# Recommendation model on one core: the hand-over from the GRU to the AUGRU, with two key steps and the first gates moved ahead of the branch

## The chip, the core and the metric

The kernel runs on one core of a Trainium2 chip. A core has a matmul engine (TensorE, "PE" in the profile, with weight loads shown apart as "PEld"), a vector engine (VectorE, "DVE"), an activation engine (ScalarE, "ACT"), a general engine (GpSimd, "POOL") and a queue that issues transfers (SyncE, "SP"). The metric is the device time in microseconds (us) of one execution. The kernel before was timed in three runs: 2016.58, 2017.4 and 2022.05 us, median 2017.4.

## The reference

1024 users each have a history of 100 items of 128 values, a mask and a length. Cut to what matters:

```python
_, gru_seq = lax.scan(gru_step, h0, swapaxes(item_historical_embedding, 0, 1))
keys = swapaxes(gru_seq, 0, 1)                       # (1024, 100, 128)
q = broadcast_to(item_embedding[:, None, :], keys.shape)
feat = concatenate([keys, q, keys - q, q * keys], axis=-1)
score = mlp(feat, [(att_W0, att_b0), (att_W1, att_b1), (att_W2, att_b2)], relu)
attn = softmax(where(mask[:, :, None] == 1, score, -inf), axis=1)[..., 0]
pooled = einsum('bt,btd->bd', attn, keys)
att_seq = pooled.T[:T]                               # AUGRU's weights: step t uses pooled[:, t]
# AUGRU step, x_t = keys[:, t], a_t = att_seq[t]:
r = sigmoid([h, x_t] @ aug_Wr.T + aug_br)
u = a_t * sigmoid([h, x_t] @ aug_Wu.T + aug_bu)
h_hat = tanh([h * r, x_t] @ aug_Wh.T + aug_bh)
h = (1 - u) * h + u * h_hat
attention_feature = aug_out[b, sequential_length[b] - 1]
comb = concatenate([user, item, hist_sum, item * hist_sum, attention_feature], axis=1)
return mlp(comb, [(ph_W0, ph_b0), (ph_W1, ph_b1), (ph_W2, ph_b2)], sigmoid)[:, 0]
```

The AUGRU can't start before the softmax over all 100 steps is known, since its first weight is a column of `pooled`.

## The kernel before

Everything is float32. Values lie with the 128 features on the partitions and users along the free dimension, in two halves of 512 users (`HB`). The program has two parts: `gru_phase`, and after a branch `augru_phase`, of which three bodies exist for three tables of step widths. The number that chooses the body, `over_d`, is computed early in the GRU part and read by every engine when it reaches the branch.

**The loop of the GRU part** runs over the steps s = 0 to 99. In a step each half goes through `gru` (gates on PE, sigmoid and tanh on ACT, the state update on DVE), the previous state is transposed into a key tile `kt` on DVE (`transpose`) and stored to `keys_d` every four steps (`store`), and the attention net runs behind the recurrence: `attend(t)` is one round of PE work on four 32-column groups of the array, in which the first layer of step t, the second layer of step t - 1 and the third layer of step t - 2 run together, since `w12` holds the later layers in the column groups that the first layer leaves free. The first layer's input is `hn` (the key) and `kq` (key times item). Its item part is constant over the steps: it was computed once as `q0` (`item_part`), with the bias in it, and `take(t)` adds it: DVE writes `f = pm + q0` (line 734), ACT writes `mv = relu(f)` (line 739). `take` then sends the score row of step t - 2 to `s_b`, four copies for the four partition quarters, on the SP queue (line 746).

The softmax runs online in blocks that end at `ENDS`: the last three blocks are the steps 93 to 95 (called A here), 96 and 97 (B), 98 and 99 (C). Each block is three stages: `scores(0)` (transposes `s_b`, masks), `tops` (`scores(1)` and the running maximum), and, after the exponential on ACT (`exponents`), `sums` (mask, sum, the new denominator: lines 809 to 823). `pool` then rescales the accumulator `pooled` (line 626) and adds key times weight for each step (lines 636 and 637): for half 0 on POOL, for half 1 on DVE in the last stretch.

**The tail of the GRU part** follows the loop, written out by hand, from `gather_early(4)` on. It runs the attention rounds 99, 100 and 101 (`T` is 100), the softmax of A, B and C, and the last pooling. Between them stand: the eight parts of the prediction net's first layer that don't depend on the AUGRU (`features`, called `some(...)`: matmuls of line 667 on the first `next`, the copy of line 675 on the second; `features` 3 and 7 issue a store to `part_d`), the stores of the last key tiles (line 609), and indirect gathers of sorted key rows on POOL (`gather_early`, line 188). At the end DVE multiplies `pooled` with a mask into `s_b` (line 978), half 1 first, and SP writes it to `pooled_d`: columns 0 to 31 to `pooled_d[0]` (line 982), the other three quarters to `pooled_d[1]`: half 1's by SP (line 987), half 0's by ACT, in the AUGRU part (line 1410).

**The AUGRU part** begins on PE with the keys of steps 0 and 1, gathered long before as `rows[0, i]`: `load_key` transposes them on PE (line 1110) and copies them out on ACT (line 1111). `first_step` computes the gates of step 0, which need no state (lines 1030 and 1032). POOL gathers the sorted weights `att_r` from `pooled_d[0]`, four gathers for each half (`gather_weights`, line 153), and then the rows of two more blocks of keys (`load_row(1, 0, k)` for k = 14 and 15). PE spreads a weight column over the partitions (`weight_row`, line 1053, tiles `first` and `spare`), DVE makes the first state (lines 1064 and 1065), and the steps follow (`half_step`, lines 1127 and 1131 on PE). Later gathers of POOL are paced by a copy that waits for a state of the running step (line 187). `gather_more` takes the other three quarters of the weights from `pooled_d[1]` after step 4.

The queues matter here: each engine runs its instructions in the order of the program, SP issues its transfers in order, and POOL issues its gathers one after the other. PSUM banks of the tail: `banks` holds two for the softmax (`e`), one each for `kw` and `pt`, two for the features (`f`); the pool `pa` has two more, for the attention rounds.

Of the kernel before, what the change touches and what calls it, by code (L numbers as in the profile page):

```python
# [83 lines left out]
def kernel(ctx: ExitStack, tc: tile.TileContext, a: dict, out: bass.AP):  # L84
# [114 lines left out]
    def gru_phase(pools):  # L199
# [491 lines left out]
        def attend(t):  # L691
# [17 lines left out]

            for turn in range(2 * NH):  # L710
                i, j = divmod(turn, 2)
                for q in range(2):
                    first(i, q, j)
# [10 lines left out]
        def take(t):  # L724
# [6 lines left out]
            for half in halves:  # L731
                if t < T:
                    sums.append(wp.tile([P, HB], F32, name="f"))
                    nc.vector.tensor_add(sums[-1], p[half.i], q0[:, half.cols])
            for half in halves:
                half.mv = wp.tile([P, HB], F32, name="mv", bufs=4)
                to, of, bias = half.mv[rows, :], p[half.i][rows, :], bm[half.i][rows, :]
                if t < T:
# [19 lines left out]
        def softmax():  # L758
# [49 lines left out]
            def sums():  # L808
                nc.vector.tensor_mul(e[:, :, :n], e[:, :, :n], on)  # L809
                nc.vector.tensor_reduce(den_n, e[:, :, :n], AX.X, ALU.add)  # L810
                if j:
                    old = sp.tile([P, NK], F32, name="old")
                    nc.vector.tensor_mul(old, den_old, e[:, :, n])
# [120 lines left out]
        some(2, 3)  # L934
        take(T - 1)
        some(2, 3)
        attend(T)
        some(4)
# [3 lines left out]
        n = ENDS[-3] - ENDS[-4] + 1  # L942
        copy = banks["e"][0][:, : NK * n].rearrange("p (k n) -> p k n", n=n)
        nc.vector.tensor_copy(copy, weights[:, :, :n])
# [8 lines left out]
        some(4)  # L953
        attend(T + 1)
        some(5, 6)
        stage()
        take(T + 1)
        exponents()
        some(5, 6)
        some(7)  # L960
        for half in halves:
            half.store((T - 1) // G)
        halves[1].pool(T, nc.vector)
        stage()
        gather_early(3)
        halves[0].pool(T, nc.gpsimd)
        some(7)
        stage(2)
        exponents()
        stage()  # L970
# [15 lines left out]
        for to, t in later["att", 1]:  # L986
            nc.sync.dma_start(out=to, in_=t)

    def augru_phase(pools, widths, alive):
# [4 lines left out]
        fp = pools.enter_context(tc.tile_pool(name="fp3", bufs=NH))  # L994
# [24 lines left out]

        def first_step(i):  # L1020

            k = keys.pop((0, i))
            gates = []
            for j, (n, f) in enumerate((("u", AF.Sigmoid), ("h", AF.Tanh))):

                if j:
                    p = pa.tile([P, HB], F32, tag="a", name=f"p{n}")
                else:
                    p = bank(f"p{n}", FREE_BANK)
                nc.tensor.matmul(p, lhsT=later["w" + n][:, 1, :], rhs=k, start=True, stop=True)  # L1030
                gate = fp.tile([P, HB], F32, name=f"first_{n}")
                nc.scalar.activation(gate, p, f, bias=later["b" + n])
# [524 lines left out]
```

## Time and profile before

| what | value | from |
|---|---|---|
| median of the timed runs | 2017.4 us | times |
| the profiled execution | 2009.0 us, span 2007.1 us | times, page |
| PE, DVE, ACT, POOL busy | 99%, 83%, 47%, 63% of the span | page, part 1 |
| mean granted PE clock | 0.995 | cores |
| last gate matmul of the GRU loop starts | 1374.75 us | timeline of PE |
| first matmul of the AUGRU part (line 1110) | 1405.47 us | timeline of PE |
| first state gate (line 1131) | 1427.69 us | timeline of PE |
| AUGRU steps follow each other without a gap from | 1432.89 us | timeline of PE |
| 1378.7 to 1432.9 us: PE, DVE, ACT, POOL busy | 42.36, 35.38, 20.96, 41.37 of 54.20 us | stretches |

A busy share is an average over the whole span; the change touches only the stretch from about 1374 to 1433 us, 3% of it. There PE isn't busy throughout: it has the gap ahead of 1405.47 us and several waits after it. A line of the timeline gives the start in us, the duration, the engine, the line of the program, the operation, output and inputs, and how many instructions are merged; brackets hold the idle time ahead of it and what ended that. A line of the chain of waits gives the start, the duration and the work or transfer that the next piece waited for.

### The profile page before, as it was taken

To read this page: it belongs to the slowest core of one execution; us is meant where nothing else is said; L and a number is where in the kernel's file an instruction comes from. 1 tells how busy PE (TensorE), PEld (TensorE's weight loads), DVE (VectorE), ACT (ScalarE), POOL (GpSimd) and SP (SyncE) were. 2 spreads that over 40 slices of the span, in tenths; PEclk is the share of its full clock that TensorE was granted. 3 is DMA by queue.
4 is the path that set the end of the run, shared out by engine and by line. 5 is a ranking of instruction groups with operands and counts; after the bars stand their busy time and mean duration, and the time that the engine had idled before them with its cause. 6 is when DMAs were issued, how large, how long until landed. Compare 5 with 4: busy or idle time off the path is not lost. (4 is left out here: it accounts for less than half of the span.)

```text
span 2007.1 us, 41031 instructions
## 1 busy us (share of the span) xinstructions
PE 1983.7 (99%) x15380; PEld 994.6 (50%) x15380; DVE 1671.7 (83%) x3010; ACT 934.8 (47%) x1672; POOL 1274.2 (63%) x1325
## 2 busy tenths in 40 slices
PE   9999999999999999999999999998899999999998
PEld 2334444444444444444444444434444556678997
DVE  7878999887978888888878798998577777888985
ACT  4444454454544454544444454554343444444553
POOL 0233939669796959496896868898774353445331
PEclk9999999999999999999999999999999999999998
DMA  4443333333334434333333333333443343333331
GB/s 125 98 118 92 107 99 106 91 83 106 115 106 109 121 103 125 115 104 102 103 105 106 107 92 107 108 91 94 123 132 99 94 112 95 93 101 99 84 79 32
DMA packets 242075, 204.85 MB, mean 102 GB/s; under 512 B 59506, under 2 KB 204890, under 8 KB 241866
## 3 DMA queue, kind: packets, MB, share of 16 engines
q1 hardware_dynamic: 227514, 169.37, 30.2%
q0 software_dynamic: 12480, 32.04, 5.8%
q8 instruction: 123, 2.02, 0.4%
q10 hardware_dynamic: 1872, 0.72, 0.1%
q14 instruction: 86, 0.70, 0.1%
HBM read 146.01 MB, written 54.41 MB: 100 GB/s over the span
## 5 line engine op out<-in xcount | busy, mean ns | idle before, releaser
L534 PE MATMUL ps<-x,wih 128*32 128x512 f32 x4800 | 616.3, 593 | 0.0
L534 PE MATMUL ps<-hn,whh 128*32 128x512 f32 x4752 | 610.7, 592 | 1.4 <-ACT hn L582 1.4
L534 PEld LDWEIGHTS ps<-x,wih 128*32 128x32 f32 x4800 | 216.1, 110 | 302.0 <-issue 298.7
L534 PEld LDWEIGHTS ps<-hn,whh 128*32 128x32 f32 x4752 | 214.3, 110 | 298.9 <-issue 295.3
L519 POOL TENSOR_TENSOR xm<-x,m 128x512 f32<-128x512 f32 x200 | 234.9, 1174 | 143.2 <-DMA m<-mask_d 142.9
L546 ACT ACTIVATE r<-ps,brz 128x512 f32<-128x512 f32 x200 | 137.7, 689 | 386.3 <-PE ps L534 386.1
L520 POOL TENSOR_TENSOR hist<-hist,xm 128x512 f32<-128x512 f32 x200 | 257.9, 1290 | 15.7
L188 POOL DMA_INDIRECT rows<-keys_d,idx_k x218 | 211.5, 970 | 80.7 <-POOL rows L187 72.5
L637 POOL TENSOR_TENSOR pooled<-pooled,kw 128x512 f32<-128x512 f32 x191 | 245.0, 1283 | 15.0
L636 POOL TENSOR_TENSOR kw<-kt,e 128x512 f32<-128x512 f32 x191 | 206.2, 1080 | 69.7 <-DVE e L809 69.6
L565 ACT ACTIVATE ps<-ps,bih 128x512 f32<-128x512 f32 x200 | 132.4, 662 | 229.4 <-DVE ps L564 229.4
L700 PE MATMUL pm<-hn,wk 128*32 128x512 f32 x1200 | 221.8, 592 | 0.0
L700 PE MATMUL pm<-kq,wkq 128*32 128x512 f32 x1200 | 221.7, 592 | 0.0
L1139 ACT ACTIVATE c<-ph,bh 128x510 f32<-128x510 f32 (+57 forms) x174 | 88.3, 507 | 261.1 <-PE ph L1131 261.0
L554 DVE SCALAR_TENSOR_TENSOR u<-ps,bhh,r 128x512 f32<-128x512 f32 x198 | 147.5, 745 | 71.3 <-PE ps L534 68.6
L700 PE MATMUL pm<-mv,w 128*32 128x512 f32 (+1 forms) x808 | 195.4, 592 | 0.6 <-DVE e L790 0.6
L569 DVE TENSOR_TENSOR d<-hn,ps 128x512 f32<-128x512 f32 x198 | 136.1, 687 | 35.9 <-ACT ps L565 35.7
L564 DVE TENSOR_TENSOR ps<-ps,u 128x512 f32<-128x512 f32 x200 | 140.0, 700 | 25.9 <-remote 4.5
L582 ACT COPY hn<-ps 128x512 f32<-128x512 f32 x200 | 116.6, 583 | 93.5 <-DVE kq L576 91.8
L570 DVE TENSOR_TENSOR d<-ps,d 128x512 f32<-128x512 f32 x200 | 138.4, 692 | 26.0 <-ACT ps L566 11.6
L187 POOL COPY rows<-rest 128x1 f32<-128x1 f32 x202 | 38.4, 190 | 175.4 <-DVE rest L1168 170.0
L571 DVE TENSOR_TENSOR ps<-ps,d 128x512 f32<-128x512 f32 x200 | 139.9, 700 | 6.8
(224 smaller groups left out, 3111.8 us busy)
## 6 DMA issues: line engine op xcount, KB each, us to landing
x<-in_hist_x SPq DMA_DIRECT2D x210, 256.0 KB
keys_d<-kt SPq DMA_DIRECT2D x48, 1024.0 KB
m<-mask_d SPq DMA_DIRECT2D x200, 128.0 KB
rows<-keys_d,idx_k POOLq DMA_INDIRECT x218, 3.0
s_b<-mv SPq DMA_DIRECT2D x200, 8.0 KB
keys_d<-kt SPq DMA_DIRECT2D x32, 64.0 KB
mask_i<-in_mask SPq DMA_DIRECT2D x8, 200.0 KB
part_d<-part SPq DMA_DIRECT2D x2, 400.0 KB
```

What stands on the lines that cost most here:

```text
L188: nc.gpsimd.indirect_dma_start(out=r[:, at, :], out_offset=None, in_=keys_d[q], in_offset=bass.IndirectOffsetOnAxis(ap=idx_k[:, k, i : i + ...
L519: nc.gpsimd.tensor_mul(d, x, m)
L520: nc.gpsimd.tensor_add(acc, acc, d)
L534: nc.tensor.matmul(p[ts(q, R), :], lhsT=w[:, g, ts(q, R)], rhs=v, start=(j == 0), stop=(j == len(parts) - 1),)
L546: nc.scalar.activation(r, pr, AF.Sigmoid, bias=brz[:, 0:1])
L554: nc.vector.scalar_tensor_tensor(out=u, in0=ph, scalar=bhh[:, 2:3], in1=r, op0=ALU.add, op1=ALU.mult,)
L564: nc.vector.tensor_add(pi, pi, u)
L570: nc.vector.tensor_mul(d, pz, d)
L571: nc.vector.tensor_add(pi, pi, d)
L636: eng.tensor_mul(d, k, w)
L637: eng.tensor_add(acc, acc, d)
L700: nc.tensor.matmul(p[i][s, :], lhsT=w[:, s], rhs=v, start=start, stop=stop)
```

## The change

Four things are changed.

- **The attention rounds 98 and 99** (`T - 2 <= t < T`) get the item part as matmuls of `wq` and `item`, accumulated into the same PSUM tile (`query`: six more packs in a round, two for each half in the column groups 0 and 1, and one for each half in the group that `QB` names). `take` then no longer adds `q0` on DVE for these two rounds; ACT applies the bias and relu from PSUM.
- **The tail** is put in another order. Features are issued one at a time in other places (`some(2)`, `some(3)`, `some(4, 5)`, `some(6, 7)`), B's exponential comes ahead of `take(T + 1)`, half 1's pooling is cut in three (1, then 2, then the rest), `gather_early` runs 2 + 3 instead of 3 + 3 times, and the stores of the last key tiles come after the second part store. In A's `sums` the weights are first copied to PSUM, and the sum and the scaled old denominator are taken from there; the copy that stood after A's `sums` (line 944) goes.
- **The keys of steps 0 and 1** are transposed and copied in the tail, into `h3` and `hist`, and the **gates of step 0** are computed there, into `item` and the unused pair of `s_b`. `first_step`, its pool and the two key loads leave the AUGRU part.
- **The stores to `pooled_d[1]`** leave the hand-over: SP issues them in step 2 of the AUGRU, three after each half's step. One more key row gather (k = 13) comes behind the weight gathers.

```diff
--- before.py
+++ after.py
@@ -707,8 +707,17 @@
             def more(i, q):
                 pack(i, q, w12[i][k_rows, :], old[i][k_rows, :], True, q == QA[i] or t >= T)
 
+            def query(i, *groups):
+                for q in groups:
+                    pack(i, q, wq[i], item[:, halves[i].cols], False, False)
+
             for turn in range(2 * NH):
                 i, j = divmod(turn, 2)
+                if j and T - 2 <= t < T:
+                    query(i, 0, 1)
+                    if i:
+                        query(1, QB[1])
+                        query(0, QB[0])
                 for q in range(2):
                     first(i, q, j)
                 if i == 0:
@@ -729,13 +738,13 @@
             rows = slice(0 if t < T else 2 * R, P)
             sums = []
             for half in halves:
-                if t < T:
+                if t < T - 2:
                     sums.append(wp.tile([P, HB], F32, name="f"))
                     nc.vector.tensor_add(sums[-1], p[half.i], q0[:, half.cols])
             for half in halves:
                 half.mv = wp.tile([P, HB], F32, name="mv", bufs=4)
                 to, of, bias = half.mv[rows, :], p[half.i][rows, :], bm[half.i][rows, :]
-                if t < T:
+                if t < T - 2:
                     nc.scalar.activation(to, sums[half.i], AF.Relu)
                 else:
                     nc.scalar.activation(to, of, AF.Relu, bias=bias)
@@ -807,10 +816,17 @@
 
             def sums():
                 nc.vector.tensor_mul(e[:, :, :n], e[:, :, :n], on)
-                nc.vector.tensor_reduce(den_n, e[:, :, :n], AX.X, ALU.add)
+                f, old = e, None
+                if banks and both[1] is None:
+                    b = banks["e"][0]
+                    f = soft["copy"] = b[:, : NK * rows].rearrange("p (k n) -> p k n", n=rows)
+                    old = b[:, HB - NK :]
+                    nc.vector.tensor_copy(f, e[:, :, :rows])
+                nc.vector.tensor_reduce(den_n, f[:, :, :n], AX.X, ALU.add)
                 if j:
-                    old = sp.tile([P, NK], F32, name="old")
-                    nc.vector.tensor_mul(old, den_old, e[:, :, n])
+                    if old is None:
+                        old = sp.tile([P, NK], F32, name="old")
+                    nc.vector.tensor_mul(old, den_old, f[:, :, n])
                     nc.vector.tensor_add(den, den_n, old)
                 if last:
                     nc.vector.reciprocal(den, den)
@@ -931,17 +947,15 @@
         weights = soft["e"][0]
         exponents()
         some(0, 1)
-        some(2, 3)
+        some(2)
         take(T - 1)
-        some(2, 3)
+        some(2)
         attend(T)
-        some(4)
+        some(3)
         for half in halves:
             half.transpose(T - 1)
         stage()
-        n = ENDS[-3] - ENDS[-4] + 1
-        copy = banks["e"][0][:, : NK * n].rearrange("p (k n) -> p k n", n=n)
-        nc.vector.tensor_copy(copy, weights[:, :, :n])
+        copy = soft["copy"]
         for half in halves:
             half.todo = [
                 ((w[0], copy if w[0] is weights else None), n, t) for w, n, t in half.todo
@@ -950,23 +964,50 @@
         halves[1].pool(1, nc.vector)
         stage()
         take(T)
-        some(4)
+        some(3)
         attend(T + 1)
-        some(5, 6)
+        some(4, 5)
         stage()
+        exponents()
         take(T + 1)
-        exponents()
-        some(5, 6)
-        some(7)
+        some(4, 5)
+        some(6, 7)
+        halves[1].pool(1, nc.vector)
+        stage()
+        halves[0].pool(T, nc.gpsimd)
+        gather_early(2)
+        halves[1].pool(2, nc.vector)
+        some(6, 7)
+        for n in range(2):
+            for half in halves:
+                k = (h3[half.i], hist[:, half.cols])[n]
+                p = pa.tile([P, HB], F32, tag="a", name="pk")
+                for g in range(GH):
+                    nc.tensor.transpose(
+                        p[:, ts(g, P)], rows[0, half.i][:, g, ts(n, P)], ident
+                    )
+                nc.scalar.copy(k, p)
+                later["key", n, half.i] = k
         for half in halves:
             half.store((T - 1) // G)
-        halves[1].pool(T, nc.vector)
-        stage()
-        gather_early(3)
-        halves[0].pool(T, nc.gpsimd)
-        some(7)
         stage(2)
         exponents()
+        for half in halves:
+            gates = (item[:, half.cols], s_bs[NH * ((soft["j"] - 1) % 2) + half.i])
+            later["gates", half.i] = gates
+            for to, (n, f) in zip(gates, (("u", AF.Sigmoid), ("h", AF.Tanh))):
+                if half.i:
+                    p = banks["f"].pop(0)
+                else:
+                    p = pa.tile([P, HB], F32, tag="a", name=f"p{n}")
+                nc.tensor.matmul(
+                    p,
+                    lhsT=later["w" + n][:, 1, :],
+                    rhs=later["key", 0, half.i],
+                    start=True,
+                    stop=True,
+                )
+                nc.scalar.activation(to, p, f, bias=later["b" + n])
         stage()
         halves[0].pool(T, nc.gpsimd)
         halves[1].pool(T, nc.vector)
@@ -983,15 +1024,12 @@
             later["att", half.i] = [
                 (others[p - 1], t[p * R : (p + 1) * R]) for p in range(1, P // R)
             ]
-        for to, t in later["att", 1]:
-            nc.sync.dma_start(out=to, in_=t)
 
     def augru_phase(pools, widths, alive):
 
 
 
         qp = pools.enter_context(tc.tile_pool(name="qp3", bufs=4 * NH))
-        fp = pools.enter_context(tc.tile_pool(name="fp3", bufs=NH))
         wp = pools.enter_context(tc.tile_pool(name="wp3", bufs=3))
         sp = pools.enter_context(tc.tile_pool(name="sp3", bufs=2))
         kp = pools.enter_context(tc.tile_pool(name="kp3", bufs=4))
@@ -1016,22 +1054,6 @@
                 n = ring.pop(0)
                 ring.append(n)
             return ps[n].tile([P, HB], F32, tag="g", name=name)
-
-        def first_step(i):
-
-            k = keys.pop((0, i))
-            gates = []
-            for j, (n, f) in enumerate((("u", AF.Sigmoid), ("h", AF.Tanh))):
-
-                if j:
-                    p = pa.tile([P, HB], F32, tag="a", name=f"p{n}")
-                else:
-                    p = bank(f"p{n}", FREE_BANK)
-                nc.tensor.matmul(p, lhsT=later["w" + n][:, 1, :], rhs=k, start=True, stop=True)
-                gate = fp.tile([P, HB], F32, name=f"first_{n}")
-                nc.scalar.activation(gate, p, f, bias=later["b" + n])
-                gates.append(gate)
-            return gates
 
         def gather_weights(i):
             r = wp.tile([P, GH, P], F32, tag="att_r", name="att_r", bufs=2)
@@ -1401,15 +1423,10 @@
             return [b - a for a, b in zip(done, done[1:])]
 
 
-        for i in range(NH):
-            load_key(0, i, (None, FREE_BANK)[i])
-        gates = [first_step(i) for i in range(NH)]
-        for i in range(NH):
-            load_key(1, i, (FREE_BANK, None)[i])
-        for to, t in later["att", 0]:
-            nc.scalar.dma_start(out=to, in_=t)
+        gates = [later["gates", i] for i in range(NH)]
+        keys.update({(1, i): later["key", 1, i] for i in range(NH)})
         sorted_rows = [gather_weights(i) for i in range(NH)]
-        for k in range(14, KH):
+        for k in range(13, KH):
             load_row(1, 0, k)
         for i in range(NH):
             load_key(2, i, (FREE_BANK, None)[i])
@@ -1438,6 +1455,9 @@
                     whole_step(t)
                 for _ in range(due.pop(0) if due else 0):
                     next(ahead, None)
+                if t == FIRST[1] - 2:
+                    for to, of in later["att", i]:
+                        nc.sync.dma_start(out=to, in_=of)
                 if t > FIRST[1]:
                     next(more, None)
                 if t == FIRST[2]:
```

## The prediction

> **What bounds the kernel now.** I read the chain of waits first, since it says which part of the hand-over sets the end. In order of time (start, duration, work) it begins so:
>
> ```profile
> 1427.23 3.61 DMA att_r<-pooled_d,idx
> ...
> 1430.89 0.50 PE spare L1053 x2
> ...
> 1432.89 1.12 PE pr L1131 x2
> ```
>
> The last of the eight weight gathers lands at 1430.84 us, PE spreads the weight, DVE makes half 1's state, and from 1432.89 all the rest of the chain is PE. So a shift of this landing is a shift of the end, one for one. What ended the waits ahead of it stands in the timelines of POOL and SP:
>
> ```profile
> 1411.35 1.27 POOL L637 TENSOR_TENSOR pooled<-pooled,kw 128x512 f32<-128x512 f32 x1
> ...
> 1415.32 0.95 POOL L188 DMA_INDIRECT rows<-keys_d,idx_k  x1 [0.30 <-DMA rows<-keys_d,idx_k]
> 1418.45 0.95 POOL L153 DMA_INDIRECT att_r<-pooled_d,idx  x1 [2.17 <-DMA pooled_d<-s_b]
> ```
>
> ```profile
> 1397.13 3.22 SPq L609 DMA_DIRECT2D keys_d<-kt  x2
> 1400.44 5.13 SPq L677 DMA_DIRECT2D part_d<-part  x1
> 1413.55 0.93 SPq L982 DMA_DIRECT2D pooled_d<-s_b  x2
> ```
>
> POOL was free at 1416.27 and waited for the two writes of `pooled_d[0]`, the second issued at 1414.15 (1413.55 and 0.6 on). These wait for DVE's last two products, and DVE's timeline shows it closed from 1386.46 on:
>
> ```profile
> 1386.46 1.29 DVE L734 TENSOR_TENSOR f<-pm,q 128x512 f32<-128x512 f32 x2 [1.52 <-PE pm L700]
> ...
> 1389.31 1.02 DVE L813 TENSOR_TENSOR old<-den,e 128x32 f32<-128x32 f32 x1
> 1390.37 1.29 DVE L814 TENSOR_TENSOR den<-den,old 128x32 f32<-128x32 f32 x1
> ...
> 1393.90 0.72 DVE L786 STREAM_TRANSPOSE last<-s_b 128x512 f32<-128x512 f32 x1
> ...
> 1400.65 0.71 DVE L786 STREAM_TRANSPOSE last<-s_b 128x512 f32<-128x512 f32 x1
> ...
> 1412.83 1.29 DVE L978 TENSOR_TENSOR s_b<-used,pooled 128x512 f32<-128x512 uint8 x2
> ```
>
> So the hand-over is DVE's line of work, then a write, then eight gathers. Beside it PE has a path of its own:
>
> ```profile
> 1389.81 1.91 PE L700 MATMUL pm<-mv,w 128*32 128x512 f32 x8
> ...
> 1405.47 1.94 PE L1110 MATMUL pk<-ident,rows 128*128 128x128 f32 x8 [6.10 <-issue]
> ...
> 1424.92 1.16 PE L1053 MATMUL first<-ident,att_r 128*128 128x128 f32 x8 [0.72 <-ACT k L1111]
> ```
>
> It stands 6.10 us at the branch, and its first weight spread waited for a key copy, not for a gather: this path is nearly as long as the other.
>
> **Step 1, the item part on PE.** Round 100's row above holds two packs after each other in each of two column groups: 1.91 us, 0.85 a pack and 0.2 to drain. The six new packs put two more on groups 0 and 1, so a round gets 1.7 us longer; bounds 0.85 (the second pair runs beside others) and 2.55 (three batches). Round 98 starts at 1374.35 and the features behind it at 1378.70, now 1380.4; they take 2.9 (to 1381.61), so round 99 starts at 1383.3. It took 4.74 (1381.61 to 1386.35), with a wait for `mv`, which ACT finished at 1382.69; that is now early. Unhindered it is 4 x 0.85 + 0.2 = 3.6, with the packs 5.3: it ends at 1388.6, 2.25 later than before.
>
> **Step 2, what DVE is spared.** Four `f` adds (1381.94 - 1380.74 and the row of 1386.46): 2.5 us, and the 1.52 of waiting. A's `sums` with the copy took from 1388.89 to 1391.86, 2.97 us; the two small products in it lasted 1.02 and 1.29, while B's on PSUM operands took 0.19 each. With the copy at 0.28 the new one is 1.3 us: 1.7 less. DVE ends its last loop product at 1380.82, the first stages of A (3.0) at 1383.8, ACT loads its table and takes the exponential (1.6, both key transposes beneath it) to 1385.5, `sums` to 1386.8, one pooling piece (2.1) to 1388.9. From there B's scores could start, 5.0 us ahead of 1393.90.
>
> **Step 3, where PE takes it back.** B's scores need the row of step 97, out of round 99. ACT takes relu straight from PSUM (1.26 by the rows of rounds 100 and 101): 1388.7 to 1389.95, where before it ended at 1388.42. The write before was issued for half 1 at 1388.44 and moved its last bytes at 1389.8 (transfers in slices of 0.1 us). So half 0's row is there at 1390.9: B starts at 1391.1, 2.8 ahead of before, after 2.2 us of idle DVE. Ends: 1388.9 to 1392.8.
>
> **Step 4, to the last product.** B's two stages take 3.04 (1393.90 to 1396.94), one pooling piece 1.44, B's `sums` 1.1, two pieces and a rescale 3.55: C's scores at 1400.3. Its row is ready: rounds 100 and 101 end at 1391.95 and 1395.3, the relu at 1396.65, the write at 1398.1. C's stages 3.04, exponential 0.3, `sums` 1.93: 1405.6, only 0.3 ahead of 1405.92, since 3.5 us of half 1's pooling now stand ahead of it. POOL takes B at 1396.9 (5.82, as from 1400.89 to 1406.71), two gathers 2.5, C at 1405.7 (5.83): half 0 is pooled at 1411.5, 1.1 earlier. DVE ends half 1 at 1410.6 and waits for POOL; the last product ends at 1412.3, 1.8 earlier than 1414.12.
>
> **Step 5, write and gathers.** From the second write to the first gather took 4.3 us (1414.15 to 1418.45). With 4.3 again the gathers start at 1416.65, 1.8 earlier. POOL is done with its three row gathers at 1415.1 and would allow 3.3. The six writes to `pooled_d[1]` are out of the way, which speaks for less than 4.3; the key stores, moved from 1397 to about 1401.8, speak for more. Transfers were at 90% or more from 1398.3 to 1408; shifted and short of one gather that is 1402.6 to 1412, and SP, whose next issue behind two stores took 5.13 us, is free again by then. I keep 4.3; ends 2.8 and 6.5 (the landing of a row gather in that full stretch). Eight gathers take 8.78 from first to last start, and the last lands 2.5 to 3.6 later (the seven others, the chain's row): 1427.9 to 1429.0.
>
> **Step 6, PE's path.** Features 6 and 7 end at about 1400.7, the four keys with their copies (0.45 and 0.58 each) at 1403.2, four gates at 0.86 at 1406.6: all this lies under DVE's line and costs nothing unless PE arrives late. It then meets the branch: 6.1 us as before, with transfers as full as before, so 1412.7. From the keys of step 2 to the first weight spread it took 9.2 us (1415.72 to 1424.92). The stretches show the clock that part of this will run at (PE, PEld, DVE, ACT, POOL, clock, transfers, GB/s):
>
> ```profile
> 1401.90:1405.40 3.50, 0.00 (x0) 0.00 (x0) 2.85 (x13) 0.23 (x1) 3.38 (x4) 0.50 1.09 322
> 1405.40:1408.00 2.60, 1.94 (x8) 1.57 (x8) 2.50 (x6) 0.00 (x0) 2.49 (x3) 0.50 0.88 273
> 1408.00:1412.10 4.10, 2.97 (x4) 1.29 (x5) 3.94 (x6) 3.04 (x4) 3.94 (x4) 0.50 0.04 14
> 1412.10:1415.00 2.90, 2.84 (x9) 1.09 (x8) 1.98 (x3) 1.84 (x3) 2.45 (x3) 0.99 0.17 37
> ```
>
> Half speed came 2.5 us after PE's last matmul and lasted until 6.6 us after its first. The same after the new gap, at a busy share of 0.75 (4.91 of 6.7 us), costs 6.6 x 0.75 / 2 = 2.5: first spread at 1424.4. From it to the spread for half 1 took 5.0 (1424.92 to 1429.94): 1429.4. Ends: 1426.9 without any slow clock, 1429.7 with all 6.6 us busy.
>
> [...]
>
> **The small moves.** The six writes at step 2 cost SP some 3.6 us (1.88 for three, ACT's 1.69). Behind them on SP wait only weight loads for two steps later, with 10.1 us a step (half 0's gate at 1444.53 and 1454.62). The one more row gather is 1.26 of POOL after the eighth; POOL then stood idle 3.86 until 1434.56. Without that cover it costs 1.26.
>
> **Sum.** The start of the closed run follows the later of 1427.9 to 1429.0 and 1429.4: 1429.4 against 1430.84, 1.4 us less. The profiled execution took 2009.0 (span 2007.1): 2007.6. The timed median is 8.4 above the profiled execution; that offset kept, 2017.4 - 1.4 = 2016.0. The ends of steps 3, 5 and 6 together give -3.3 to +0.6: 2014.1 to 2018.0.
>
> **Rivals.** *DVE's line comes through whole*: packs at the low end, B at 1388.9. Then POOL is bound by its own work (1394.8 after A, 5.82, 2.5, 5.83: 1409), and the branch must be shorter as well. Some 4 us less: 2013.4. For it: the 5.0 of step 2 are sure; against: round 99 and PE's path. *No change*: PE's branch and slow clock, or the same landing, keep 1430.8; within 0.6 of 2017.4. For it: the 0.72 row, where PE was late already. *Slower, by the moved key stores*: they still fill the transfers when `pooled_d[0]` is written. A write that then takes as long as a row gather in the full stretch, 6.5 instead of 2.6, starts the gathers at 1420.5, 2.1 after before: 2019.5. It decides from where the stores last beyond about 1414; 1412 is my sum, so it is near. Against: some 4 us of quiet transfers between 1409.5 and the first write at 1413.55 before.
>
> **Numbers.** Forecast 0.5, whole line 0.14, no change 0.22, slower 0.14. A difference of 0.3%, 6.05 us, is about what a measurement of this kernel can tell from no change; no case reaches it alone, but the timed runs spread by 5.5 us. Faster than 2011.3: 0.10, within: 0.82, slower than 2023.4: 0.08. Range 2011 to 2021: the cases' ends 2013.4 and 2019.5, and some 2 us of that spread.
>
> **What would show it.** Right: 12 more records in rounds 98 and 99, no `f` in the tail, DVE idle ahead of B's first transpose at about 1391, the small sums at 0.2, the first weight gather near 1416.6, and PE closed from about 1431.5. Wrong: B's first transpose without a wait (step 3), transfers at 90% beyond 1413 (step 5), the gap at PE's branch under 4 us or the first weight spread waiting for a gather (step 6), a stall in steps 2 to 5.

## The result and the profile after

| | before | after |
|---|---|---|
| median of 14 runs each | 2019.01 us (2016.58 to 2022.05) | 2018.73 us (2015.81 to 2021.3) |
| ratio, 95% interval | | 0.9998 [0.9991, 1.0005] |
| profiled execution, span | 2009.0, 2007.1 us | 2018.55, 2016.7 us |
| granted PE clock of that execution | 0.995 | 0.993 |

No difference could be measured: -0.3 us, with an interval from -1.8 to +1.0. The kernel before took about 2019 us in three of the five series of runs here and about 2007.6 us in the two others, and its first profile (2009.0 us) is near the second, so a time is compared only with before's in its own series. In the traces I count from a common point, the last gate matmul of the GRU loop (1374.75 us before, 1374.83 after).

The chain of waits of the kernel after, in order of time (start, duration, what), goes over PE, ACT and the branch ("issue"), where that of before went over the last weight gather:

```profile
1401.43 0.67 PE pk L986 x4
...
1407.25 3.86 issue
1411.11 1.94 PE pk L1132 x8
...
1421.24 0.58 ACT k L1133
...
1424.72 1.12 PE pr L1153 x2
...
1427.98 0.59 ACT at L1092
...
1432.34 0.66 DVE att_t L1100
...
1434.39 1.12 PE pr L1153 x2
```

No transfer is on it any more: the tail is quicker, and the weights are there when PE asks. The first state gate starts at 1424.72 (before 1427.69), yet the closed run (the stretch from which PE's steps follow each other without a gap) starts at 1434.39, 1.5 us after before's 1432.89. So 3.0 us were won, and 4.5 lost in the first half step.

DVE's timeline shows the tail:

```profile
1385.81 0.30 DVE L824 COPY last<-e 128x128 f32<-128x128 f32 x1
...
1386.44 0.20 DVE L829 TENSOR_TENSOR last<-den,last 128x32 f32<-128x32 f32 x1
...
1390.64 0.73 DVE L795 STREAM_TRANSPOSE last<-s_b 128x512 f32<-128x512 f32 x1 [1.86 <-DMA s_b<-mv]
...
1403.43 0.23 DVE L818 TENSOR_TENSOR last<-last,on 128x64 f32<-128x64 f32 x1 [1.06 <-ACT last L815]
...
1412.07 0.69 DVE L1019 TENSOR_TENSOR s_b<-used,pooled 128x512 f32<-128x512 uint8 x1 [1.16 <-POOL pooled L637]
```

The copy and the short sums are as cheap as on PSUM before (0.30 and 0.20, where before had 0.28 and 0.19 there; `old` took 1.02), B's first transpose waits 1.86 us for its row, and the last product waits for POOL. One wait is new: C's products wait 1.06 us for ACT, whose exponential stands behind the copies of the moved keys.

SP's queue and POOL's timeline show the write and the first gather:

```profile
1401.18 3.12 SPq L609 DMA_DIRECT2D keys_d<-kt  x2
1410.94 2.18 SPq L1023 DMA_DIRECT2D pooled_d<-s_b  x2
```

```profile
1415.18 0.95 POOL L188 DMA_INDIRECT rows<-keys_d,idx_k  x1 [0.30 <-DMA rows<-keys_d,idx_k]
1416.44 0.95 POOL L153 DMA_INDIRECT att_r<-pooled_d,idx  x1 [0.30 <-issue]
```

The first weight gather (1418.45 before, behind a wait of 2.17 for the write) follows POOL's own gathers of rows with 0.30 between, as they follow each other. PE's timeline shows its own path:

```profile
1382.59 0.62 PE L700 MATMUL pm<-hn,wk 128*32 128x512 f32 x2
...
1386.51 1.42 PE L700 MATMUL pm<-kq,wkq 128*32 128x512 f32 x6
...
1411.11 1.94 PE L1132 MATMUL pk<-ident,rows 128*128 128x128 f32 x8 [4.59 <-issue]
...
1421.87 1.23 PE L1075 MATMUL first<-ident,att_r 128*128 128x128 f32 x8 [0.67 <-ACT k L1133]
```

Round 99 is bounded by the first two. The gap at the branch is 4.59 us where it was 6.10, and the first weight spread still waits for the copy of a key, not for a gather.

What eats the gain stands side by side in the timelines of PE and ACT in the first half step:

```profile
1425.67 1.02 PE L1153 MATMUL pu<-h_all,wu 128*128 128x510 f32 x2
1426.53 0.60 PE L1098 MATMUL pw<-ident,att_r 128*32 128x128 f32 x4
1428.62 1.16 PE L1075 MATMUL spare<-ident,att_r 128*128 128x128 f32 x8 [1.49 <-ACT at L1092]
```

```profile
1427.98 0.58 ACT L1092 COPY at<-spare 128x512 f32<-128x512 f32 x1 [6.16 <-PE pw L1098]
1429.39 0.66 ACT L1173 ACTIVATE pr<-pr,br 128x510 f32<-128x510 f32 x1 [0.82 <-PE spare L1075]
1432.18 0.66 ACT L1174 ACTIVATE pu<-pu,bu 128x510 f32<-128x510 f32 x1 [2.14 <-PE ph L1153]
```

ACT's sigmoid of `pu` starts at 1432.18, 5.5 us after the matmuls of `pu` ended (1426.69), and ACT had been idle 2.14. Its copy of `spare` starts 4.0 us after the spreads that it reads. The semaphore records of PE agree: ten of its signals come within 0.35 us from 1432.16 on. PE's signals, not its matmuls, are late there. "Late signals" below means this: engines that wait for PE start microseconds after its matmuls have ended.

### The profile page after: what moved, and what is told of

It is laid out like the page before. It is cut to its first block, busy times and chain, and to the rows that moved or that the text cites. A ratio compares the mean times of both kernels' runs of the same rounds, so it can differ in the third digit from the quotient of the medians.

```text
span 2016.7 us, 41069 instructions
## 1 busy us (share of the span) xinstructions
PE 1989.9 (99%) x15404; PEld 1006.2 (50%) x15404; DVE 1666.0 (83%) x3006; ACT 934.0 (46%) x1672; POOL 1277.2 (63%) x1325
## 4 chain that ended last, share of the span: by engine, by line
PE 96%; DVE 2%; ACT 1%; issue 1%; DVEq 0%; ACTq 0%
PE ps L534 49%; PE pm L700 17%; PE ph L1153 5%; PE pr L1149 4%; PE pr L1153 4%; PE pu L1153 4%; PE ph L1149 4%; PE pu L1149 4%; PE last L667 1%; PE pr L1226 0%; PE ph L1226 0%; PE pu L1226 0%; PE p L1313 0%; PE p L1308 0%; PE p L1354 0%
## 5 line engine op out<-in xcount | busy, mean ns | idle before, releaser
L1177 DVE TENSOR_TENSOR pu<-pu,c 128x510 f32<-128x510 f32 (+57 forms) x173 | 81.9, 473 | 77.9 <-ACT c L1161 71.9
```

## The experiments

The runs were taken in four series after the comparison above: first `r_before`, `r_after`, `gates_only` and `gates_back`, one timed run each; then `swap_banks`, `late_state`, `rows_behind` and `swap_and_rows`; then `after_5`, `swap_early_rows` and `swap_banks_2`; last `gates_back_5`. In the later three each changed kernel has 11 timed runs.

The main numbers, in us from the GRU's last gate matmul (starts of the second write to `pooled_d[0]`, the first weight gather, the first weight spread, then of state gates, in the last two columns half 0's):

| kernel | write | gather | spread | step 1, half 0 | step 1, half 1 | step 2 | step 11 |
|---|---|---|---|---|---|---|---|
| before | 39.40 | 43.70 | 50.17 | 52.95 | 58.14 | 64.69 | 152.57 |
| r_before | 39.44 | 43.89 | 50.64 | 53.41 | 60.23 | 66.77 | 154.65 |
| after | 37.96 | 41.61 | 47.04 | 49.89 | 59.56 | 66.11 | 153.99 |
| r_after | 37.97 | 41.63 | 47.43 | 50.48 | 60.72 | 67.83 | 155.71 |
| after_5 | 37.97 | 41.62 | 47.16 | 49.94 | 54.77 | 61.31 | 149.19 |
| gates_only | 40.52 | 45.04 | 50.62 | 53.39 | 61.34 | 70.73 | 158.61 |
| gates_back | 37.19 | 40.85 | 54.49 | 58.27 | 63.13 | 69.68 | 157.56 |
| gates_back_5 | 37.19 | 40.85 | 54.54 | 58.32 | 64.94 | 71.49 | 159.37 |
| swap_banks | 37.95 | 41.61 | 47.94 | 50.71 | 55.10 | 61.65 | 150.49 |
| swap_banks_2 | 37.96 | 41.61 | 48.29 | 51.06 | 55.45 | 62.00 | 150.82 |
| late_state | 37.96 | 41.62 | 47.76 | 53.47 | 61.09 | 67.63 | 155.51 |
| rows_behind | 37.96 | 41.26 | 47.63 | 50.40 | 55.23 | 61.78 | 151.44 |
| swap_and_rows | 37.96 | 41.62 | 47.77 | 50.54 | 54.93 | 61.48 | 151.37 |
| swap_early_rows | 37.96 | 41.62 | 47.92 | 50.69 | 55.08 | 61.63 | 149.51 |

**1. Both kernels once more.** No edit.

> The kernel before once more, for a profile beside that of the kernel after. Two spans are counted from the last gate matmul of the GRU loop: to the first state gate of the AUGRU (52.9 us in the first profile) and to its closed run, the first PE work behind the first state of half 1 (58.1 us). If the hand-over is the same in every execution, both repeat within 0.3 us. If it varies from run to run by more than 1 us, the difference of 1.5 us between the two profiles says nothing.

> The changed kernel once more. Its profile has the first state gate 49.9 us after the loop and the closed run 59.6 us after it: 3.0 us won and then 4.5 us lost in the first half step, in which ACT and DVE start some 4 us after PE's matmuls have ended. Theory 1, the loss belongs to the new order: both spans repeat within 0.3 us. Theory 2, it is an accident of that execution: the first span repeats, the closed run comes at 55.0 us, 5.1 after the first state gate as in the kernel before.

One run each, 2016.08 and 2018.52 us, beside 2019.94 for another run of before: too few to rank. Up to the gathers each kernel repeats itself within 0.2 us, and the first state gate of the change is 2.9 us earlier (50.48 against 53.41). From it to half 1's took 10.24 us in the change; in the kernel before 6.82, where its first profile has 5.19. So the late signals aren't the change's own: a second profile of before has them as well, for less time. The gain up to the first state gate repeats, and half 1's gate isn't earlier.

**2. The moved gates alone, on the kernel before.**

```diff
+        for n in range(2):
+            for half in halves:
+                k = (h3[half.i], hist[:, half.cols])[n]
...
-        gates = [first_step(i) for i in range(NH)]
+        gates = [later["gates", i] for i in range(NH)]
```

> The kernel before with one part of the change alone: keys of steps 0 and 1 and the gates of step 0 ahead of the branch. DVE's line of work is that of before. If that line and the gathers behind it set the start, the first state gate stays at 52.9 and the closed run at 58.1, within 0.5 us. If PE's own path set it (its first weight spread waited 0.72 us for a key copy), up to 0.7 us are won. If the new entry itself brings the late half step of the changed kernel, the closed run is some 9.5 us after the first state gate instead of 5.2.

2021.42 us in one run, beside 2019.94 for before. The first state gate is no earlier than before's (53.39), and half 1's is 3.2 us later than in the first profile of before, with late signals. But the write, 1.1 us later than before's, was late already ahead of everything that was moved. Round 99's last matmul ended at 1385.42, and DVE's sum of it began 1.2 us after that, where before it took 0.11:

```profile
1386.62 1.29 DVE L734 TENSOR_TENSOR f<-pm,q 128x512 f32<-128x512 f32 x2 [2.67 <-PE pm L700]
```

PE's time saved is then spent waiting: 2.93 us for a copy of a key, which ACT made behind its three stores to `pooled_d[1]` (issued from 1414.31 on), and these wait for DVE's last product. So DVE's line holds this start, but how much the moved gates would win without the 1.1 us can't be read from this one profile. The trace of before gives a bound: its fourth weight gather starts at 1422.21, the gathers land 2.4 to 2.6 us after their start, so half 0's last weights are there at about 1424.7 (an estimate), and the spread that needs them ran from 1424.92 to 1426.08. A shorter path of PE alone could win about 1 us there, not 3.

**3. The change without the moved gates.** The same diff the other way round, on the kernel after: its tail, with the keys and the first gates behind the branch.

> The changed kernel with the keys and the first gates back behind the branch, all else as changed. The weight gathers start some 1.9 us earlier than before, but PE has its old path behind the branch: if that path binds, the first state gate is at 52.5 to 53 us, and the closed run at 57.5 to 58.1. If the gathers alone bind, 50 to 51 and 56. If the late half step comes from the tail or the stores and not from the entry, it is here too: 9.5 us from the first state gate to the closed run.

> The changed kernel with the keys of steps 0 and 1 and the first gates put back behind the branch, once more, timed: the tail is then as quick as in the changed kernel, and PE's own work behind the branch is that of before. Theory D (what binds the first state gate is the later of two lines: the tail with its weight gathers, and PE's own keys and gates behind the branch; the change shortens both and neither alone pays): the second write at 37.2 us from the GRU's last gate matmul as in the changed kernel, the first spread at 50 to 54.5 behind PE's own work with no wait for a gather, half 0's first state gate at 53 to 58 (before 52.95, changed 49.9), time 0 to 3 us over the kernel before. Rival (the tail alone binds, and PE's moved keys only fill idle time): first spread at 47 to 48, the gate at 50 to 51, time 1 to 3 us below before as with the whole change.

One run of 2017.58 us, and timed later 2021.56 against 2018.63, ratio 1.0015 [1.0006, 1.0024]: 2.9 us slower, beyond its interval. The write is 2.2 us earlier than in before and the gathers 2.9, but the first spread is at 54.5 in both profiles, 4 us later than before's. PE's timeline of the second, and a row of ACT's, show for what it waits:

```profile
1408.69 2.08 PE L1043 MATMUL pu<-k,wu 128*128 128x512 f32 x2 [5.71 <-ACT k L1124]
...
1425.62 0.66 PE L1123 MATMUL pk<-ident,rows 128*128 128x128 f32 x4 [1.84 <-issue]
1427.82 1.55 PE L1066 MATMUL first<-ident,att_r 128*128 128x128 f32 x8 [1.54 <-ACT k L1124]
```

```profile
1407.57 1.07 ACT L1124 COPY k<-pk 128x512 f32<-128x512 f32 x2 [6.48 <-issue]
```

It waits for its own keys; the last of the eight gathers had started at 1422.91. But this isn't before's path of PE with a shorter tail: the first copy of a key stands on ACT 6.48 us behind its last work, with no wait that the profile shows, and PE's first gate waits 5.71 us for it (1.73 in before); the half clock lasts 13.7 us (10.2 in before). So half 0's gate is at 58.3, 5 us later than the 52.5 to 53 that the first expectation gave to a binding path of PE. What the runs and the bound above show is that each line holds the start when only the other is shortened: the shorter tail with the old entry gives nothing, the moved gates alone at most about 1 us, and both together bring the first gate 3 us forward. Why ACT's copy comes so late there stays open.

**4. Step 1 with two uses of a bank exchanged.** On the kernel after:

```diff
-                store_weights(0, pa.tile([P, HB], F32, tag="a", name="pw"))
-                first_state(1, spare)
+                first_state(1, pa.tile([P, HB], F32, tag="a", name="first"))
+                store_weights(0, spare)
```

> The changed kernel with two of step 1's uses of a PSUM bank exchanged: half 1's first-state weights are spread into the bank that half 0's first state has just left, and the transposes for the store of half 0's weights go into the bank `spare`. In the changed kernel PE's spread for half 1 stands behind a copy on ScalarE (of `spare` into `at`) that began 4.0 us (5.8 in the repeat) after PE had ended what it reads. All spans from the last gate matmul of the GRU. Theory A (the first half step is long because half 1's spread waits for that copy, and VectorE's copy of `pw` stands ahead of half 1's state): half 1's first state gate, at 59.6 and 60.7 in the two profiles of the changed kernel, comes some 5 to 6 us behind half 0's (49.9 and 50.5), so at 55 to 57, and the kernel is 3 to 5 us quicker than the changed one. Theory B (what PE has done is told late to the other engines at this place of the program, whatever the order): ACT and DVE begin step 1's sigmoids and products 3 to 6 us after the matmuls they read, half 1's gate stays at 58.5 to 61, and the time is within 1.5 us of the changed kernel's 2018.7.

> The exchange of banks alone once more, beside the other two: half 1's first state gate 0.3 to 0.6 us earlier than in the changed kernel where the signals aren't late, time 0 to 1.5 us below it. If the late signals show in this call, the gate is at 58 to 61 in all three, and the exchange didn't remove them.

Ratios 0.9993 [0.9984, 1.0002] and 0.9998 [0.9989, 1.0007]. In both series the late signals were gone from every profile, in that of the unedited kernel too (run 5), so these runs can't say whether the exchange would cure them. What it gives without them: 4.39 us from gate to gate in both against 4.83 in `after_5`, so 0.4 us, not the 3 to 5 that theory A expected from the first profiles. And it was given back: PE waits in step 4, and DVE's timeline shows the cause:

```profile
1457.11 1.10 PE L1149 MATMUL pr<-k,wr 128*128 128x496 f32 x2 [0.69 <-DVE k L1139]
```

```profile
1456.34 1.30 DVE L1139 STREAM_TRANSPOSE k<-rows 128x512 f32<-128x512 f32 x2 [2.40 <-DMA rows<-keys_d,idx_k]
```

A gather of rows is late. POOL issues one per 1.44 us, each paced by a copy of `rest`, which DVE makes later here, behind half 1's state: the first paced copy is at 57.3 us from the common point, in `after_5` at 56.4.

**5. The change itself, without late signals.** No edit.

> The changed kernel once more, to see where its gain goes on a chip on which the signals of PE aren't late (or to see them late again). All spans from the last gate matmul of the GRU. Theory C (the gain is real up to step 1, and POOL's gathers of rows take part of it back before step 4): first state gate of half 0 at 50.4, of half 1 at 55.0 to 55.5 (52.95 and 58.14 in the profile of before), PE waits 0.7 to 1.8 us for VectorE's `k`, which waits for a gather of rows, ahead of the keys' gates of step 4, and from there on the lead is 1.1 to 2.1 us; the time is 0.5 to 3 us below that of the kernel before on the same chip. Theory B (late signals, whatever the order): half 1's gate at 59 to 61 again, no wait for `k` at step 4, time equal to before's within 1.5 us.

2005.21 us against 2007.54, ratio 0.9988 [0.9979, 0.9997]: 2.3 us faster, with an interval that just leaves out no change. PE's timeline and ACT's show the first half step as it was planned:

```profile
1424.32 1.12 PE L1153 MATMUL pr<-h_all,wr 128*128 128x510 f32 x2 [0.72 <-DVE h_all L1087]
1425.27 1.02 PE L1153 MATMUL pu<-h_all,wu 128*128 128x510 f32 x2
...
1429.14 1.12 PE L1153 MATMUL pr<-h_all,wr 128*128 128x510 f32 x2 [0.66 <-DVE h_all L1087]
```

```profile
1426.33 0.66 ACT L1174 ACTIVATE pu<-pu,bu 128x510 f32<-128x510 f32 x1 [0.20 <-PE pu L1153]
```

ACT takes `pu` as soon as it is there, where it stood at 5.5 us in the first profile. Half 1's gate comes 3.4 us earlier than in the undisturbed profile of before (54.77 against 58.14), and at step 11 the lead is 3.4 still. The wait in step 4 that theory C expected isn't there: the same gather held DVE for only 0.74 us, and PE not at all.

**6. Four copies on VectorE ahead of half 0's first state.** On the kernel after:

```diff
             nc.vector.tensor_mul(p, p, u)
+            for _ in range(4 if i == 0 else 0):
+                nc.vector.tensor_copy(p, p)
             nc.vector.tensor_mul(h3[i], p, h)
```

> The changed kernel with four copies of a 128x512 tile in place on VectorE (0.69 us each, 2.8 us in all) between the two products of half 0's first state: what the change won at the first state gate (3.0 us) is given back there by hand. The result is the same. Theory A (step 1 is a chain that begins with the first state gate): half 0's gate goes from 49.9-50.5 us to 52.7-53.3, half 1's from 59.6-60.7 to 62.4-63.5, and the kernel is 2.8 us slower than the changed one. Theory B (the late signals hold the start of the closed run at one place, whatever is ready before): half 0's gate moves by 2.8, half 1's stays within 1 us of 59.6-60.7, and the time is that of the changed kernel within 1 us.

2010.29 us, ratio to before 1.0013 [1.0004, 1.0022]. Half 1's gate at 61.09 is near what both theories wrote, since both had built on the profiles with late signals; against `after_5`, the right base, it is 6.3 us later for 2.9 us of copies (0.6 of it from a first spread that came later), and the medians of the two kernels differ by 5.1 with before alike in their series (2007.7 and 2007.54). Theory B, which needs late signals, isn't put to the test; without them the start follows half 0's gate, and the cost is twice what theory A said. PE's timeline shows why:

```profile
1428.26 2.07 PE L1155 MATMUL pr<-h_all,wr 128*128 128x510 f32 x2 [3.66 <-DVE h_all L1089]
1430.12 1.91 PE L1155 MATMUL pu<-h_all,wu 128*128 128x510 f32 x2
```

After an idle stretch of 3.66 us the pairs that take 1.12 and 1.02 take 2.07 and 1.91; the granted clock is 0.50 from 1427.2 to 1434.0. The half clock began 2.6 us after PE's last matmul (1424.60); in `gates_only` the gap of 2.93 us was followed by half clock too, from 1417.1 to 1420.5.

**7. The last three gathers of rows behind the weight gathers.** On the kernel after, alone and with the exchange of run 4:

```diff
-        gather_early(3)
...
-        for k in range(13, KH):
+        for k in range(10, KH):
```

> The changed kernel with the three gathers of rows that close the hand-over moved behind the eight gathers of attention weights. The first weight gather began 3.65 us after the second write's issue in the changed kernel and 4.30 in the kernel before, with no wait on it that the profile shows (0.30, issue): theory A (POOL's own three gathers set it) puts it up to 1.1 us earlier, at about 40.5 us from the last gate matmul of the GRU instead of 41.6, and the eighth gather at 49.3 instead of 50.4; the first spread is bound by PE's own path (the copy of key 3 on ScalarE) and moves by less than 0.7, so the time stays within 1 us of the changed kernel's. Theory B (the write's landing sets it): the first gather stays at 41.6 within 0.2. Both say the same for the time; a gain over 1.5 us would say that the weight gathers do bind the start.

> The two edits together, the exchange of banks and the rows behind the weights, on the changed kernel. If the exchange frees half 1's spread (theory A of the exchange), the eighth weight gather is the next thing that half 1 waits for, and the two together give 3 to 6 us over the changed kernel (2013 to 2016 against 2018.7). If the signals are late whatever the order (theory B), the time is within 1.5 us of the changed kernel's.

Ratios 0.9997 [0.9988, 1.0006] and 0.9998 [0.9989, 1.0007]. The first gather began at 41.26 and 41.62 instead of 41.62, now after a wait of 4.05 and 4.41 us for the write: the write lands at most 0.4 us before POOL is done with its rows, and there is next to nothing to win. PE's wait in step 4 was 1.52 us in the first of them, and the lead at step 11 fell to 1.1 us.

**8. Four more gathers of rows ahead of step 1.** The kernel of run 4, and:

```diff
-        due = spread_over(-(-widths[FIRST[1]] // R), NH * (FIRST[1] - 2))
+        due = spread_over(-(-widths[FIRST[1]] // R) - 4, NH * (FIRST[1] - 2))
+        for _ in range(4):
+            next(ahead)
```

> The changed kernel with the banks of step 1 exchanged as above and with four of the gathers of rows for the keys of step 4 issued ahead of step 1, without the copy that paces them, where POOL had 2.2 us (6.0 in the changed kernel) of idle time. Theory C (the start of the closed run is held by POOL's gathers of rows at step 4, 1.44 us for each with its pacing copy): the wait of 0.69 us of PE for `k` that the exchange alone showed ahead of step 4 goes, and the lead that the exchange has at step 2 (3.0 us on the kernel before) stays to the narrow steps, 0.96 us more than it kept; time 1 us below that of the exchange alone and 2 to 4 below before's. Rival (the gathers share the queue with step 2's weights and keys, so early ones delay the loads of `at` or the weight gathers): half 1's first state gate later than 55.1 by 0.5 or more, and no gain.

2005.25 us, ratio 0.9988 [0.9979, 0.9997]. DVE's transposes of step 4 no longer wait:

```profile
1454.46 1.30 DVE L1139 STREAM_TRANSPOSE k<-rows 128x512 f32<-128x512 f32 x2
```

The 3.1 us of lead at step 2 are there at step 11 too (149.51 against 152.57); the exchange alone had 2.7 at step 2 and kept 1.8 in the same series. Half 1's gate stayed at 55.1. So the gathers of rows are what held step 4. In time the kernel equals the change (2005.21 in the same series); no version beat it measurably.

**What hides a microsecond or two here.** The narrow last steps run partly at half clock. The stretches at the end of the kernel after and of `after_5` (PE, PEld, DVE, ACT, POOL, clock, transfers, GB/s):

```profile
1999.10:2016.70 17.60, 13.24 (x60) 10.94 (x60) 4.10 (x19) 4.03 (x13) 0.64 (x1) 0.50 0.07 14
```

```profile
1992.10:2003.50 11.40, 7.05 (x32) 4.76 (x31) 2.00 (x8) 2.25 (x7) 0.00 (x0) 0.50 0.00 0
```

It begins 17.6 us ahead of the end in one and 11.4 in the other. Of the 33 runs of before in the series with `late_state`, the seven at a mean clock of 0.993 took 2010.8 to 2011.6 us, the six at 0.997 took 2004.4 to 2005.9: the 7 us spread goes with the clock, whichever causes the other, and a gain of 2 us must be seen through it.

## Why the prediction was right, and where its steps were off

The forecast of 2016.0, 1.4 us below before, stands within what was measured: -0.3 us (-1.8 to +1.0) in the first comparison, -2.3 (-4.2 to -0.6) in the series of `after_5`. That the difference would be hard to tell from none was right. So was the mechanism, two lines that must both get shorter: in the kernel after, the tail and PE's path are both earlier, and runs 2 and 3 with the bound from before's gathers show that neither does it alone. The size is another matter. Without late signals the start is 3.4 us earlier, with them not earlier at all, and 1.4 lies between the two by errors that partly cancel.

- **Step 1** was mis-sized. Round 98 got 0.9 us longer instead of 1.7 (it starts 0.08 later, and the features behind it at 1379.68, before 1378.70): the packs on the two column groups run largely beside others, and the low bound of 0.85 was the nearer. Round 99 took 5.3 us as predicted, from an earlier start, but by luck: by round 98 (4.35 us before, 5.25 with the packs) it is 4.4 and 0.9, not the predicted 3.6 and 1.7.
- **Steps 2 and 3** were right: no `f`, small sums at 0.2, B's first transpose at 1390.64 (predicted 1391.1) behind an idle stretch of DVE of 1.9 us (2.2).
- **Step 4** was right to half a microsecond: POOL's last pooling ended at 1412.04 (1411.5), the last product at 1412.76 (1412.3). It left out that C's exponential queues behind the copies of the moved keys on ACT; part of that 1.06 us wait is the exponential itself (0.25).
- **Step 5** was right in its result (first gather 1416.44, predicted 1416.65) and wrong in its reason. Write to gather took 3.65 us instead of 4.3, and the end is set by POOL's three gathers of rows, which the prediction had ready at 1415.1; they were 1.0 later than that, after a last pooling product of 1.68 us (1.27 before) and a first gather of 1.43 (0.99). Run 7 puts the landing 0 to 0.4 us ahead of them. The rival of the moved key stores needed transfers beyond 1414, and the transfers, at 0.35 of the engines from 1411 to 1414, show that they weren't in the way.
- **Step 6** named the right line, PE's own, and made it too long. The gap at the branch was 4.59 us instead of "6.1 us as before", and from there to the first spread took 10.8 instead of 11.7. The spread came at 1421.87, not 1424.4, and half 0's gate 3.0 us earlier than before. The half clock lasted 6.8 us, 10.2 before. The upper end of this step is also wrong by its own sum: all 6.6 us busy cost 3.3, which gives 1430.2 and not 1429.7.
- **The sum** went from half 0's spread to half 1's by before's 5.0. That holds without late signals: 5.03 in `after_5` (1421.54 to 1426.57), and the closed run starts at 1429.14 (1429.5 in before's count) instead of the predicted 1431.5. But it set unlike points against each other: 1429.4 is the start of that spread, which before started at 1429.94, and 1430.84 is the landing for which only its last matmuls waited. From start to start its own steps give 0.5 us, not 1.4.
- **Late signals** made the spreads 6.8 us apart in the kernel after, and the closed run came 5.8 after the second, against 3.0 before. Of that the prediction had nothing. It is the likely reason why the first comparison shows no gain: with late signals in both kernels, the change stands 0.7 us ahead of `r_before` at step 11 in one profile (153.99 against 154.65) and 1.1 behind in the other (155.71). That rests on one profile of before and two of the change; the other timed runs have no trace.
- **The small moves** were right that nothing in steps 2 to 5 stalls by the six writes or the one gather. But the cover was thin: the "3.86 of idle POOL" was the wait for step 1, which shrinks when step 1 comes earlier. In `after_5` a gather of rows held DVE for 0.74 us in step 4 already, and 0.9 us later ones (the exchange) held PE for 0.7. The price of the uncovered gather was named; the point from which it counts wasn't.
- Of the rivals, *no change* has the first comparison's time, though probably by late signals, and not by the same branch or landing; *DVE's line whole* falls with B's wait of 1.86 us.

## What to carry to other kernels

Where two lines meet at a start, shorten both or expect nothing: the shorter tail with the old entry gave a slower kernel here (1.0015), both together the gain. When one part is tried alone, compare the traces ahead of the edit too: in run 2 the 1.1 us of the write were lost before anything that was moved. Take the lead at several points after the edit (first gate, second step, tenth), since what was won at one can be gone at the next, and ask which background work, sized for the old start, becomes the next wait. A time near the noise needs the mean clock of each run beside it.

## What was not expected of the hardware

- PE's signals were late by up to 5.8 us at the start of the AUGRU part. Bursts of five to ten signals within 0.35 us stand there in `after` and in the five profiles of the first and the last series (in `gates_back` and `gates_back_5` with little effect), and in none of the eight others. The same six profiles, and no other, have such bursts again between 1942 and 1968 us, in the narrow steps, so neither the branch nor the new entry is needed for them. PE's starts show what they go with: `r_before` falls 2.1 us behind before's first profile at the hand-over, another 4.1 between 1920 and 1968, and 2.6 from there to the end. The same six profiles also lack some 12% of all semaphore records (22395 to 22692, where the others have 25567 to 25594), nearly all of PE's missing ones from 1400 us on. What makes them late stays open; `after_5`, without them, ran on the chip of `r_after`, so it isn't the chip as such.
- An idle stretch of PE of 3.66 us, for 2.9 us of work on another engine, cost 5.7 us (6.3 less 0.6), since half the clock followed for 6.8. The stretches of half clock at the hand-over lasted 3.4 us (`gates_only`), 6.8 (after, `after_5`, `late_state`), 10.2 (before) or 13.7 (`gates_back_5`), steps of 3.4.
- The gap of PE at the branch was 4.59 us in the change and 6.10 before, with transfers about as full in the two stretches from 1401.9 to 1408.0 (0.95 and 1.02 of the engines; 1.09 and 0.88 before). It was 3.65 us in `gates_only` and 2.13 and 2.30 in the two profiles without the moved gates, where ACT stood instead. What sets its length wasn't tried.
